# Two attention layers on one core: the places at which the next pair's q, k and v are quantized in the first image's attention

## The chip, the cores and the metric

The kernel runs on one core of one Trainium2 chip. The metric is the device time of one execution in microseconds (us); the time before is the median of 3 runs. One further execution was recorded by the hardware profiler, and all profile lines come from it. Its engines are TensorE (PE, with its weight loads PEld), VectorE (DVE), ScalarE (ACT), GpSimd (POOL) and SyncE (SP), which here issues most of the DMAs.

## The reference

Two layers over 8 images of 512 channels and 1024 positions. Layer 0 is an attention with 8 heads of 64 channels whose q, k and v are each fake-quantized with one scale for the whole tensor; layer 1 is an attention with one head of 512 channels. Cut to what matters here:

```python
def fake_quant(x):                       # scale and zero point of the whole tensor
    scale = max((xmax - xmin) / 255, 1e-8)
    zp = round(-xmin / scale)
    return (clip(round(x / scale) + zp, 0, 255) - zp) * scale

# layer 0
h = group_norm(x, gn_w, gn_b)
q, k, v = split(einsum('oc,bct->bot', qkv_w, h) + qkv_b)   # per head
q, k, v = fake_quant(q), fake_quant(k), fake_quant(v)
w = softmax(einsum('bct,bcs->bts', q * s, k * s))
a = einsum('bts,bcs->bct', w, v)
x = x + einsum('oc,bct->bot', proj_w, a) + proj_b
# layer 1
t = group_norm(x, ...)
x = x + proj(softmax(q1(t) @ k1(t).T / sqrt(512)) @ v1(t))
```

## The kernel before

Since the quantizing scale needs the whole tensor, the kernel first computes q, k and v of all images, writes them to DRAM in float32 and keeps running extremes (the first 577 us of the trace). Then come layer 0's attention and layer 1. They are interleaved: the attention of image b+1 is given out in small portions between the matmuls of layer 1 of image b. For the first image there is no layer 1 to interleave with yet, and its attention runs by itself. It is accompanied only by `fold`, which multiplies layer 1's weight matrices together.

The attention works in *units*. A unit is (image b, head pair j, half hf of the queries, key tile s): 128 keys against 512 queries, for two heads at once. A pair thus has 16 units, and an image 4 pairs. For each unit:

- `scores` (TensorE): two matmuls of the pair's quantized k and q into `st`, which has two buffers; then ScalarE's exponential from `st` into `pt`, 128x1024 float32.
- `split`: `pt` is cut into two float16 parts in the tile `two`. The high part is a cast, on ScalarE, or on GpSimd where s % 4 is 2, or on VectorE where s is 5; the low part, the remainder `pt - high`, is always VectorE's. In the first image units with s % 4 of 3 are `plain`: their `pt` is used in float32 (tile `aside`) and no split is made.
- `over_keys` (TensorE): the products `av` of `two` with the quantized v (float32 `vf` for plain units). `totals` (TensorE): the row sums `sm`.

In `attention`, one turn of the loop takes four units u to u+3 through `over_keys` and `totals`, and at the same time computes the scores of units u+6 to u+9 and splits them. So scores run six to eight units ahead of the products. The first scores of the next pair therefore come in the last turns of this one.

`load_pair(b, j, u)` prepares the next pair while this one runs; u is the number of this pair's first unit. It fetches q and k (512 KB each) by SP into tiles `raw`, of which there are two, and lays out the quantizing. q, k and v each take two VectorE steps over 128x1024: `quant` (scale and round, in place in `raw`) and `quant2` (clip, into bfloat16 q and k or float16 v). v of the first image has a third, `whole`, which writes the rows of the plain units in float32 into `vf`. That makes seven steps. `fetch_v` loads v into the tile that q has left; the next pair's q then goes into k's tile and its k into v's.

What sets the order of this work depends on the phase. In the first image's attention, `InOrder.strict` is set and `InOrder.planned` is not: the instructions on each engine stay in the order in which the program writes them. Small pieces of work wait in the list `dealt`, each with the number of the unit from which it may go. Each `split(u)` calls `deal(u)`, which takes one piece, the first in the list whose number has been reached (and `fetch_v` with it if it stands next). In this way the quantizing steps, the divide by the row sums (`ao`), the sums' reciprocals (`rcs`) and steps of `fold` are scattered among the remainders on VectorE. `settle("qk")` in `scores` gives out whatever of q and k is left when a new pair begins; `settle("qv")` does it for v.

For later images, `InOrder.planned` is set: a planner with costs and due times orders the same work through `dve.later`. SP's DMAs, too, run in order of its queue; a load waits there until its tile is free, and what stands behind it waits as well.

## Time and profile before

| | us |
|---|---|
| median of 3 runs (lowest, highest) | 2619.14 (2615.93, 2619.39) |
| profiled execution, its own time | 2616.86 |
| span of its trace | 2615.1 |
| TensorE busy | 2532.9, 97% |
| VectorE busy | 1905.7, 73% |
| ScalarE busy | 1360.2, 52% |
| GpSimd busy | 189.2, 7% |
| mean granted TensorE clock | 0.989 of full |
| first scores of the first image | 585.62 |
| first scores of its pairs 1, 2, 3, and of the next image | 617.63, 650.79, 684.44, 717.21 |
| first projection matmul of image 0 | 741.76 |

A line of the timeline gives the start in us, the duration in us, the engine, the line of the program, the operation, the tile written and the tile read, their shapes, how many instructions are merged, and in brackets the idle time before it and what ended it. Nearly all engine instructions carry the line of a helper (L91 or L209), so they are told apart by the tiles. A line of the busy times by stretch gives the stretch, its length, the busy time of TensorE, its weight loads, VectorE, ScalarE and GpSimd with the number of instructions, the granted TensorE clock, the DMA engines' mean busy share and GB/s. Durations of one instruction overlap a little with the next one's start, so that the distance between starts is shorter than a duration.

### The profile page before, as it was taken

The page shows a single profiled execution, that of the slowest core. Times are in us where ns is not written, and L with a number is a line of the kernel's source. Part 1 is how long each engine was busy: PE and PEld are TensorE (multiplying, and loading weights), DVE is VectorE, ACT ScalarE, POOL GpSimd, SP SyncE. Part 2 cuts the span into 40 slices and gives each one's busy share as a digit, 9 for nine tenths or more (in the row PEclk, how much of TensorE's full clock was granted, in tenths as well). Part 3 has the DMA queues.
Part 4 walks back from the last instruction along what each step waited for, and adds up shares of the span by engine and source line. Part 5 has one row for each costly group of instructions (what it writes and reads, how often), then busy time and mean ns, then how long its engine had stood idle before and what let it go on. Part 6 is the DMA issues. An engine that isn't in the chain of part 4 may idle for free.

```text
span 2615.1 us, 38713 instructions
## 1 busy us (share of the span) xinstructions
PE 2532.9 (97%) x15670; PEld 1749.2 (67%) x15670; DVE 1905.7 (73%) x2748; ACT 1360.2 (52%) x1696; POOL 189.2 (7%) x153
## 2 busy tenths in 40 slices
PE   7999999997888999999999999999999999999998
PEld 4788888872235775776677577757766775777687
DVE  7888776667776777877777777778777776776544
ACT  3222222217765674666566566746665765664121
POOL 0000000001100001000100010010001000100000
PEclk9999999998899999999999999999999999999999
DMA  4343333332221232223212322322232123212211
GB/s 173 128 166 128 122 128 121 118 140 81 70 94 42 69 103 82 86 79 108 96 51 78 118 85 63 109 82 86 73 110 97 54 78 117 86 42 87 91 37 38
DMA packets 156013, 243.09 MB, mean 93 GB/s; under 512 B 26544, under 2 KB 93104, under 8 KB 154288
## 3 DMA queue, kind: packets, MB, share of 16 engines
q1 hardware_dynamic: 125264, 182.81, 21.3%
q10 hardware_dynamic: 30560, 57.71, 6.5%
q8 instruction: 125, 2.05, 0.3%
q14 instruction: 64, 0.52, 0.1%
HBM read 153.64 MB, written 86.28 MB: 92 GB/s over the span
## 4 chain that ended last, share of the span: by engine, by line
PE 86%; DVE 5%; ACT 3%; issue 2%; DMA 1%; POOL 0%; SPq 0%; ACTq 0%; DVEq 0%
PE s L209 15%; PE o L209 14%; PE qkps L209 12%; PE pj L209 8%; PE av L209 8%; PE v2ps L209 7%; PE g L209 7%; PE vps L209 6%; PE st L209 4%; PE sm L209 4%; DVE two L91 2%; ACT pt L91 1%; PE fold L209 1%; ACT two L91 0%; DVE acc L91 0%
## 5 line engine op out<-in xcount | busy, mean ns | idle before, releaser
L91 ACT ACTIVATE pt<-st,esc 128x1024 f32<-128x1024 f32 x496 | 527.8, 1114 | 367.6 <-PE st L209 351.7
L91 DVE TENSOR_TENSOR two<-pt,two 128x1024 f16<-128x1024 f32 x496 | 597.1, 1217 | 166.6 <-POOL two L1050 108.4
L91 ACT CAST two<-pt 128x1024 f16<-128x1024 f32 x358 | 362.2, 1054 | 13.6 <-PE sm L209 8.2
L1050 POOL CAST two<-pt 128x1024 f16<-128x1024 f32 x128 | 166.7, 1302 | 1568.2 <-ACT pt L91 779.8
L209 PE MATMUL av<-two,v 128*32 128x512 f16 x3968 | 248.0, 385 | 9.5 <-DVE v L91 9.5
L209 PE MATMUL s<-g,h 128*128 128x256 f32 x1024 | 233.4, 380 | 0.0
L209 PE MATMUL pj<-ao,wp 128*128 128x512 f32 x512 | 224.2, 595 | 2.4 <-DVE ao L91 2.0
L209 PEld LDWEIGHTS s<-g,h 128*128 128x128 f32 x1024 | 192.9, 190 | 31.0 <-issue 4.3
L209 PE MATMUL st<-q,k 64*128 64x512 bf16 x1024 | 165.7, 388 | 37.4 <-DVE k L91 23.3
L91 ACT ACTIVATE u_ring<-qkps,qkbt 128x512 f32<-128x512 f32 x89 | 61.1, 687 | 250.4 <-PE qkps L209 235.6
L209 PEld LDWEIGHTS <-v 128*32 128x32 f16 x3968 | 91.5, 96 | 148.8 <-issue 66.1
L209 PEld LDWEIGHTS pj<-ao,wp 128*128 128x128 f32 x512 | 96.0, 190 | 124.4 <-issue 112.5
L209 PE MATMUL s<-g,sums 128*128 128x256 f32 x768 | 178.5, 381 | 0.2 <-DVE p L91 0.2
L209 PE MATMUL o<-p,v 128*128 128x256 f32 x768 | 175.2, 382 | 1.0 <-DVE p L91 1.0
L209 PEld LDWEIGHTS o<-p,v 128*128 128x128 f32 x768 | 144.3, 190 | 27.1 <-issue 5.7
L209 PEld LDWEIGHTS s<-g,sums 128*128 128x128 f32 x768 | 144.6, 190 | 24.3 <-issue 4.1
L209 PEld LDWEIGHTS <-k 64*128 64x128 bf16 x1024 | 34.4, 94 | 169.6 <-issue 142.0
L209 PE MATMUL sm<-two,ones 128*32 128x512 f16 x1984 | 137.0, 381 | 0.0
L209 PE MATMUL qkps<-half,w_low 128*128 128x512 f32 x480 | 132.2, 398 | 2.3 <-DVE half L91 2.3
L209 PE MATMUL qkps<-half,w_high 128*128 128x512 f32 x480 | 133.7, 401 | 0.0
L209 PE MATMUL qkps<-half,w_mix 128*128 128x512 f32 x480 | 131.2, 396 | 1.1 <-DVE half L91 1.1
L209 PE MATMUL g<-h,wa 128*128 128x256 f32 x512 | 120.8, 384 | 0.0
(221 smaller groups left out, 3834.8 us busy)
## 6 DMA issues: line engine op xcount, KB each, us to landing
rs<-rs_d SPq DMA_DIRECT2D x76, 256.0 KB
x<-in_x_dram SPq DMA_DIRECT2D x32, 512.0 KB
q_d<-wa SPq DMA_DIRECT2D x32, 512.0 KB
k_d<-wa SPq DMA_DIRECT2D x32, 512.0 KB
v_d<-v_ring SPq DMA_DIRECT2D x32, 512.0 KB
raw<-q_d SPq DMA_DIRECT2D x32, 512.0 KB
raw<-k_d SPq DMA_DIRECT2D x32, 512.0 KB
x_d<-h SPq DMA_DIRECT2D x64, 256.0 KB
```

The source lines that it names most:

```text
L91: ins = self.latest = op(*args, **kw).ins
L209: ins = nc.tensor.matmul(ps, lhsT=lhsT, rhs=rhs, **kw).ins
L1050: copy(two[:, 0], pt)
```

## The change

Three numbers in `quants`, in the branch that is taken when the work is dealt out in program order. q's two steps move from splits 12 and 13 after the pair's start to 7 and 8, k's from 14 and 15 to 9 and 10, and v's three from 19, 20 and 21 to 15, 16 and 17. `fetch_v`, which goes with q's second step, moves from 13 to 8. The branch serves the first image's attention, that is, the steps for its pairs 1 to 3 and for the first pair of the next image.

```diff
@@ -969,9 +969,9 @@
                     if u is None or InOrder.planned:
                         dve.later(name, 0.7, work, pe.t + 12.0, 45.0)
                     else:
-                        dealt.append((u + (12, 14, 19)[i] + n, name, work))
+                        dealt.append((u + (7, 9, 15)[i] + n, name, work))
                         if (i, n) == (0, 1):
-                            dealt.append((u + 13, "qk", fetch_v))
+                            dealt.append((u + 8, "qk", fetch_v))
 
             def fetch_v():
                 if len(raws) == 2:
```

The order of instructions that follows from it: on VectorE, k's last step stands right behind the remainder of unit 10 of the pair that runs, where it stood behind the remainder of unit 14 (pairs 0 to 3; the steps for the second pair of the next image keep their places, since other pieces stand ahead of them in the list). v's steps stand around the next pair's first two remainders, where they stood around its units 2 to 4. On SP's queue, the next pair's k load comes ahead of the two loads of `h` and of the row sums' small transfers in pair 1, and ahead of the row sums' transfers in pair 2. The orders on TensorE, ScalarE and GpSimd are the same as before.

## The prediction

> **What bounds the kernel now.** I read the page first (TensorE busy 97% of the span, and 86% of the chain that ended last), then the waits of the stretch from 577 to 760 us, the only one in which the edited branch deals its work out, then the timelines of TensorE and VectorE there, and last the busy times by stretch. In the waits, the columns are total us, times, longest:

> ```profile
> ACT pt L91 <- PE st L209: 40.6, 10, 13.5
> DVE two L91 <- ACT two L91: 34.0, 13, 5.3
> ...
> PE st L209 <- DVE k L91: 23.0, 4, 5.9
> ```

> TensorE waits four times, 5.7 to 5.9 us each, for the quantized k of the next pair. ScalarE's and VectorE's long waits are the echo: while no scores come they run dry. TensorE's timeline around the second of the four, and a later piece of the same fold product:

> ```profile
> 644.24 0.61 PE L209 MATMUL sm<-two,ones 128*32 128x512 f16 x8
> 650.79 0.61 PE L209 MATMUL st<-q,k 64*128 64x512 bf16 x2 [5.95 <-DVE k L91]
> 651.33 2.08 PE L209 MATMUL fold<-wn_v 128*128 128x512 f32 x2
> ...
> 663.01 1.13 PE L209 MATMUL fold<-wn_v 128*128 128x512 f32 x2
> ```

> The fold product takes 2.08 us right after the wait and 1.13 us later. The reason is the granted clock, the last column before DMA and GB/s here; both stretches hold the same work (two scores, one fold step, one split unit and one plain unit of av, and their sums):

> ```profile
> 650.79:656.99 6.20, 6.20 (x26) 1.39 (x27) 2.06 (x2) 4.65 (x5) 0.00 (x0) 0.50 0.26 85
> 666.01:669.33 3.32, 3.32 (x30) 0.96 (x27) 3.29 (x4) 3.21 (x4) 0.83 (x1) 1.00 0.35 101
> ```

> So a wait costs twice: its own length, and then 6.20 - 3.32 = 2.88 us of half clock. VectorE's timeline shows why k is late:

> ```profile
> 644.90 1.52 DVE L91 TENSOR_SCALAR q<-raw,bhi 128x1024 bf16<-128x1024 f32 x1
> 646.34 0.68 DVE L91 CAST two<-pt 128x1024 f16<-128x1024 f32 x1
> 647.05 1.23 DVE L91 TENSOR_TENSOR two<-pt,two 128x1024 f16<-128x1024 f32 x1
> 648.19 0.75 DVE L91 TENSOR_SCALAR raw<-raw,rcp 128x1024 f32<-128x1024 f32 x1
> 648.86 1.22 DVE L91 TENSOR_TENSOR two<-pt,two 128x1024 f16<-128x1024 f32 x1
> 649.99 0.75 DVE L91 TENSOR_SCALAR k<-raw,bhi 128x1024 bf16<-128x1024 f32 x1
> 650.65 1.28 DVE L91 SCALAR_TENSOR_TENSOR ao<-ao,scl,rs 128x1024 f32<-128x1024 f32 x1
> 656.07 1.22 DVE L91 TENSOR_TENSOR two<-pt,two 128x1024 f16<-128x1024 f32 x1 [4.14 <-ACT two L91]
> ```

> When TensorE comes for k (644.85), VectorE still has six operations to do, k the last, with remainders of units 13 and 14 between them that nobody needs for another six units. It has no pause before, then 4.14 us with nothing to do. The k data are not late: their load was issued at 633.18 and the DMA went quiet by 637.

> [...] clock 0.50 after waits of 5.7 us, and none after waits of 1.1 us (at 739.03). [...] The q step above (1.52 us, not 0.75) started while GpSimd's cast of 644.53 ran[...].

> **The change, part by part.** [...] Nothing is added or removed; VectorE, ScalarE, GpSimd and TensorE run as many instructions as before. [...]

> Removed waits: 5.68 + 5.95 + 5.68 + 5.69 = 23.0 us.

> Half clock after them: from the first scores of a pair to those of units 2 and 3 the timeline takes 5.72, 6.20, 4.75 and 5.42 us; at full clock 3.32. The sum over 3.32 each is 2.40 + 2.88 + 1.43 + 2.10 = 8.8 us. TensorE alone would thus gain 31.8 us.

> It can't keep all of that, since the other engines have to follow. Busy times by pair, in the order TensorE, weights, VectorE, ScalarE, GpSimd:

> ```profile
> 585.62:617.63 32.01, 22.89 (x165) 6.58 (x164) 23.61 (x31) 25.14 (x26) 4.74 (x4) 0.87 0.12 40
> 617.63:650.79 33.16, 27.05 (x248) 8.52 (x249) 24.81 (x29) 25.40 (x28) 5.42 (x4) 0.91 0.40 128
> 650.79:684.44 33.65, 27.80 (x236) 7.92 (x237) 27.64 (x38) 25.47 (x28) 4.56 (x4) 0.86 0.26 79
> 684.44:717.21 32.77, 26.59 (x236) 7.89 (x238) 22.80 (x25) 24.71 (x27) 5.07 (x4) 0.92 0.23 66
> 717.21:741.76 24.55, 20.75 (x214) 7.18 (x214) 17.93 (x20) 22.92 (x25) 4.07 (x3) 0.91 0.27 90
> ```

> New length of each piece, as the largest of TensorE's own time and the other engines' busy time. Pair 0: 32.01 - 5.68 = 26.3. Pair 1: TensorE 33.16 - 5.95 - 2.40 = 24.8, ScalarE 25.4, VectorE 25.9 (its work counted from one pair's first remainder to the next, 622.91 to 656.07): 25.9. Pair 2: TensorE 33.65 - 5.68 - 2.88 = 25.1, VectorE 27.6: 27.6. Pair 3: TensorE 32.77 - 5.69 - 1.43 = 25.65: 25.7. The last piece: TensorE 24.55 - 2.10 = 22.45, ScalarE 22.9: 22.9. Together 128.4 against 156.1: 27.7 us. No two engines mesh without a gap, so I take off 0.5 us at each of the four pair ends (TensorE's waits inside an undisturbed pair are 0.2 to 0.6): 26 us.

> Does k come in time? The remainder of unit 10 ends, in the trace of before, 4.4, 1.75, 2.1 and 4.4 us ahead of the four waits' starts. Four quantizing steps of 0.66 (start to start) now come ahead of its successor: 2.65 us[...]. Pairs 0 and 3 keep a margin of about 1 to 1.8. In pair 1 two steps on wa (0.6 and 1.45) fall behind k, so it keeps about 1. In pair 2 nothing falls behind, and 0.6 to 1.4 us of wait stay. That is part of the 2.5 us that pair 2 has above TensorE's own time, not extra.

> What is delayed: remainders of units 8 to 10, by up to 2.65 us. Those of units 8 and 9 of pair 0 ended at 605.46 and were first read at 610.48, so 5 us are there; if that cover is gone, TensorE stands for the excess. Those of units 12 to 14 come earlier by as much.

> Loads, on SP's queue in order: v's (issued 613.29, moved by 617: 3.7 us) now follows q's second step some 10 us earlier; the next q's (617.61, done by 621) follows k. The next k's is moved past the two 1 MB loads of h and the small loads of the row sums; it waits for v's last step and makes those loads wait too. They are released by the fold's row product at 625.19 and needed for the projection at 751, so 0 us. From v's last step to k's first there are eight units, about 8 x 1.6 = 13 us, for a load of under 4: 0 us; bounds 0 and 2 us each, if h's 2 MB share the engines. [...] The divide by the row sums keeps its place behind the same DMA chain. From the projection on, the order on every engine is the old one and is only shifted.

> The sum: 2616.86 (span 2615.1 and 1.8 around it) less 26 = 2590.9. The profiled time lies below the median, 2619.14, inside the runs' 2615.93 to 2619.39; half of that offset put back gives **2592**.

> **Rivals.** (1) *VectorE takes over the wait.* At 27.6 of 27.6 us it has no slack in pair 2 and little in pair 1, so remainders come late and TensorE stands for them[...]. For it: VectorE ran without a pause from 638 to 652. Against it: its 38 us of pauses in this stretch. If two of four pair ends keep a wait of 3.5 us and 2.3 of slow clock: 26 - 11.6 = 14 us gained, 2604. (2) *Nothing moves*: something else ends the wait at the same time, such as ScalarE's exponentials, whose scores buffers are two. Against it: ScalarE itself idles 5.7 us in each of the four. 2618. (3) *Slower: the k load.* VectorE works in order, so if k's data were not there at split 9, all remainders would queue behind the step, and the pairs would be longer than now. Place: the next k's load, released by v's last step. Price: from 13 us after release on, each us costs one per pair; it eats the gain of 6.5 per pair at 19.5 and loses beyond. At 22 us, 4 x 2.5 = 10 lost: 2627. The loads seen take under 4 us, so it is remote.

> **How the numbers follow.** Forecast 0.68, own range 2587 to 2597[...]; rival 1 0.24, spread over 2597 to 2611; rival 2 0.04; rival 3 0.04. I take 2585 to 2604, which leaves out the far part of rival 1 and the last two. This kernel's measurements can tell about 0.2%, 5 us, from no change: faster 0.92, same 0.04, slower 0.04.

> **What would show it.** Right: waits of scores for k gone or under 2 us, largest at the end of pair 2; the clock near 1.00 from 600 to 740; pairs of 26 to 28 us; ScalarE and VectorE busy above nine tenths. Wrong: av products waiting for remainders by over 1 us (rival 1), a quantizing step waiting for a DMA (rival 3), or a projection that does not start about 26 us earlier than at 741.76.

## The result, and the profile after

Four runs of the changed kernel have a median of 2594.31 us (2592.55 to 2595.38), beside 2618.69 us (2615.93 to 2619.39) before: a ratio of 0.9908, 95% interval 0.9891 to 0.9925. The profiled execution took 2592.55 us against 2616.86, so 24.3 us less.

The stage in question runs from the first scores of the first image to its first projection matmul. It took 156.1 us before and takes 131.0 now. The busy times by pair of the changed kernel, in the order TensorE, weights, VectorE, ScalarE, GpSimd, then the clock (the last line is the stretch just after the end of pair 2):

```profile
585.52:611.73 26.21, 22.77 (x165) 6.58 (x165) 20.73 (x29) 24.45 (x26) 4.58 (x4) 0.87 0.21 73
611.73:637.29 25.56, 24.79 (x253) 8.19 (x250) 23.44 (x26) 25.02 (x29) 4.90 (x5) 1.00 0.43 140
637.29:666.16 28.87, 25.40 (x240) 7.75 (x237) 28.66 (x40) 25.70 (x29) 7.18 (x5) 1.00 0.27 79
666.16:693.04 26.88, 26.52 (x237) 7.78 (x238) 24.38 (x26) 24.05 (x27) 3.95 (x4) 0.94 0.40 112
693.04:716.48 23.44, 18.84 (x219) 6.88 (x215) 22.33 (x23) 23.34 (x26) 5.15 (x4) 1.00 0.23 81
...
666.16:671.07 4.91, 4.91 (x26) 1.16 (x27) 4.88 (x6) 3.48 (x4) 0.00 (x0) 0.65 0.72 216
```

The pairs took between 32.0 and 33.7 us and now take between 25.6 and 28.9. In each of the pieces at least one of TensorE, VectorE and ScalarE is now busy for over nine tenths of the time. Pair 2 is the longest, and VectorE is busy for 28.66 of its 28.87 us.

The waits of the changed kernel from 577 to 735 us, which is a little past the end of the stage:

```profile
ACT pt L91 <- PE st L209: 18.6, 6, 14.5
...
DVE two L91 <- ACT two L91: 10.7, 8, 2.9
...
ACT pt L91 <- DVE two L91: 2.9, 4, 1.4
...
PE st L209 <- DVE k L91: 1.9, 1, 1.9
```

Of the 23.0 us in which TensorE waited for k, one wait of 1.9 us is left, and the echoes on ScalarE and VectorE shrink with it. (ScalarE's longest wait, 14.5 us, lies behind the stage, where no scores are due; so did the 13.5 us before.) The third line is new in the stage: ScalarE has to wait for VectorE's remainders before it can reuse a `pt` buffer. Three of those four waits lie in pair 2; the fourth, of 0.46 us, stands behind the stage in both kernels.

TensorE's timeline at the end of pair 2, and VectorE's at the same place:

```profile
663.63 0.60 PE L209 MATMUL sm<-two,ones 128*32 128x512 f16 x8
666.16 0.39 PE L209 MATMUL st<-q,k 64*128 64x512 bf16 x2 [1.93 <-DVE k L91]
666.48 1.64 PE L209 MATMUL fold<-wn_v 128*128 128x512 f32 x2
```

```profile
662.69 1.22 DVE L91 TENSOR_TENSOR two<-pt,two 128x1024 f16<-128x1024 f32 x1
663.83 0.75 DVE L91 TENSOR_SCALAR raw<-raw,rcp 128x1024 f32<-128x1024 f32 x1
664.61 1.50 DVE L91 TENSOR_SCALAR k<-raw,bhi 128x1024 bf16<-128x1024 f32 x1
666.03 1.21 DVE L91 TENSOR_TENSOR two<-pt,two 128x1024 f16<-128x1024 f32 x1
```

VectorE's operations follow each other without a gap, and k's last step takes 1.50 us instead of 0.75: GpSimd's cast, which ran from 664.52 to 665.56, covers its start. After the wait the fold product takes 1.64 us instead of 1.12, and the clock over the next 4.91 us is 0.65.

The gain of the stage is 156.14 - 130.96 = 25.2 us. One more microsecond of it goes at the projection, where TensorE waits 1.95 us for the last `ao` in both kernels (the first line is of before, the next two are of the changed kernel):

```profile
746.56:751.50 4.94, 4.56 (x10) 1.82 (x10) 4.90 (x6) 0.00 (x0) 0.00 (x0) 1.00 0.18 53
```

```profile
716.48:734.33 17.85, 15.90 (x37) 6.51 (x34) 13.28 (x16) 3.33 (x5) 0.00 (x0) 0.90 0.38 130
721.27:726.20 4.93, 4.93 (x8) 2.15 (x9) 4.89 (x6) 0.00 (x0) 0.00 (x0) 0.65 0.19 55
```

After the same wait the clock was 1.00 before and is 0.65 now. The projection with what surrounds it, up to the next scores, takes 17.85 us where it took 16.85. So 25.2 - 1.0 = 24.2 us, and the profiled executions differ by 24.3.

### The profile page after: what moved, and what is told of

Same layout as the page of the kernel before. It is cut to its first block, busy times and chain, and to the rows that moved or that the text cites. A ratio compares the mean times of both kernels' runs of the same rounds, so it can differ in the third digit from the quotient of the medians.

```text
span 2590.7 us, 38714 instructions
## 1 busy us (share of the span) xinstructions
PE 2527.7 (98%) x15670; PEld 1749.0 (68%) x15670; DVE 1909.7 (74%) x2748; ACT 1359.1 (52%) x1696; POOL 191.0 (7%) x153
## 3 DMA queue, kind: packets, MB, share of 16 engines
q8 instruction: 125, 2.05, 0.3%
## 4 chain that ended last, share of the span: by engine, by line
PE 85%; DVE 5%; ACT 3%; issue 2%; DMA 1%; POOL 0%; ACTq 0%; SPq 0%; DVEq 0%
PE s L209 15%; PE o L209 14%; PE qkps L209 12%; PE pj L209 9%; PE av L209 8%; PE v2ps L209 7%; PE g L209 6%; PE vps L209 6%; PE st L209 4%; PE sm L209 4%; DVE two L91 2%; ACT pt L91 1%; DVE h L91 1%; PE fold L209 0%; ACT two L91 0%
## 5 line engine op out<-in xcount | busy, mean ns | idle before, releaser
L91 ACT ACTIVATE pt<-st,esc 128x1024 f32<-128x1024 f32 x496 | 528.6, 1115 | 348.0 <-PE st L209 331.0
L91 DVE TENSOR_TENSOR two<-pt,two 128x1024 f16<-128x1024 f32 x496 | 599.3, 1222 | 138.7 <-POOL two L1050 103.8
L91 ACT CAST two<-pt 128x1024 f16<-128x1024 f32 x358 | 362.4, 1055 | 13.3 <-PE sm L209 8.0
L209 PE MATMUL av<-two,v 128*32 128x512 f16 x3968 | 247.5, 384 | 9.3 <-DVE v L91 9.2
L209 PE MATMUL s<-g,h 128*128 128x256 f32 x1024 | 233.4, 380 | 0.0
L209 PE MATMUL pj<-ao,wp 128*128 128x512 f32 x512 | 225.6, 599 | 2.0 <-DVE ao L91 2.0
L209 PEld LDWEIGHTS s<-g,h 128*128 128x128 f32 x1024 | 192.9, 190 | 31.0 <-issue 4.3
L91 ACT ACTIVATE u_ring<-qkps,qkbt 128x512 f32<-128x512 f32 x89 | 61.2, 687 | 250.5 <-PE qkps L209 233.6
L209 PEld LDWEIGHTS <-v 128*32 128x32 f16 x3968 | 91.6, 96 | 147.8 <-issue 65.0
L209 PE MATMUL st<-q,k 64*128 64x512 bf16 x1024 | 164.6, 385 | 18.8 <-ACT pt L91 11.0
L209 PEld LDWEIGHTS pj<-ao,wp 128*128 128x128 f32 x512 | 96.6, 191 | 124.7 <-issue 113.1
L209 PE MATMUL s<-g,sums 128*128 128x256 f32 x768 | 178.4, 381 | 0.2 <-DVE p L91 0.2
L209 PE MATMUL o<-p,v 128*128 128x256 f32 x768 | 175.2, 382 | 1.0 <-DVE p L91 1.0
L209 PEld LDWEIGHTS o<-p,v 128*128 128x128 f32 x768 | 144.3, 190 | 27.1 <-issue 5.7
L209 PEld LDWEIGHTS s<-g,sums 128*128 128x128 f32 x768 | 144.7, 190 | 24.2 <-issue 4.1
L209 PE MATMUL sm<-two,ones 128*32 128x512 f16 x1984 | 136.7, 381 | 0.0
L209 PEld LDWEIGHTS <-k 64*128 64x128 bf16 x1024 | 34.7, 94 | 148.3 <-issue 142.0
L209 PE MATMUL qkps<-half,w_low 128*128 128x512 f32 x480 | 132.1, 398 | 2.3 <-DVE half L91 2.3
L209 PE MATMUL qkps<-half,w_high 128*128 128x512 f32 x480 | 133.9, 401 | 0.0
L209 PE MATMUL qkps<-half,w_mix 128*128 128x512 f32 x480 | 131.2, 395 | 1.1 <-DVE half L91 1.1
L209 PE MATMUL g<-h,wa 128*128 128x256 f32 x512 | 120.8, 384 | 0.0
```

The costliest lines, as they stand in the source:

```text
L91: ins = self.latest = op(*args, **kw).ins
L209: ins = nc.tensor.matmul(ps, lhsT=lhsT, rhs=rhs, **kw).ins
```

## The experiments

The median of before, run beside the first four, was 2618.69 us (19 runs); beside the next two 2617.92 (7 runs); beside the last two 2619.38 (7 runs). The time at which the first scores start differs from execution to execution, 585.2 to 589.5 us, with work that no edit here touches. The length of the stage is therefore a better measure of an edit than the total. It is read from the single profiled execution of each kernel, and the clock in it counts: the changed kernel and after_again are the same program, and their stages differ by 2.5 us.

| kernel | stage, us | its pairs 0 to 3 and last piece, us | median, us | ratio to before, 95% |
|---|---|---|---|---|
| before | 156.1 | 32.0, 33.2, 33.7, 32.8, 24.6 | 2618.69 | |
| the changed kernel | 131.0 | 26.2, 25.6, 28.9, 26.9, 23.4 | 2594.31 | 0.9908 (0.9891 to 0.9925) |
| qk_only | 131.3 | 25.0, 25.6, 31.7, 25.6, 23.5 | 2594.22 | 0.9908 (0.9891 to 0.9925) |
| v_only | 157.5 | 31.5, 32.7, 33.9, 33.9, 25.5 | 2619.89 | 1.0002 (0.9993 to 1.0011) |
| two_splits | 134.9 | 26.7, 27.7, 29.7, 27.1, 23.9 | 2597.96 | 0.9919 (0.9903 to 0.9936) |
| kept_busy | 148.7 | 31.3, 31.5, 31.3, 31.4, 23.3 | 2612.21 | 0.9974 (0.9963 to 0.9985) |
| fold_later | 129.1 | 26.4, 25.6, 26.3, 27.2, 23.6 | 2590.52 | 0.9898 (0.9882 to 0.9915) |
| fold_later_chain | 128.9 | 26.2, 25.6, 26.3, 27.2, 23.6 | 2592.15 | 0.9904 (0.9887 to 0.9920) |
| after_again | 128.5 | 25.0, 25.6, 28.9, 25.6, 23.4 | 2593.99 | 0.9902 (0.9886 to 0.9919) |
| after_filled | 130.1 | 26.1, 25.6, 28.9, 25.6, 24.0 | 2592.49 | 0.9895 (0.9879 to 0.9912) |

**Which of the moved steps carries the gain.** qk_only moves q and k and leaves v; v_only does the reverse:

```diff
-                        dealt.append((u + (12, 14, 19)[i] + n, name, work))
+                        dealt.append((u + (7, 9, 19)[i] + n, name, work))
                         if (i, n) == (0, 1):
-                            dealt.append((u + 13, "qk", fetch_v))
+                            dealt.append((u + 8, "qk", fetch_v))
```

> The changed kernel with v's three steps back at splits 19 to 21; q, k and the v load stay at their new places. My theory: all of the gain comes from k being ready, so the four waits of scores for k stay under 2.5 us, and the stretch from the first scores of image 0 (585.5) to its first projection matmul takes 129 to 133 us (before 156.1, changed 131.0); time within 3 us of the changed kernel's. Rival (the earlier v belongs to it, since the next pair's k loads into the tile that v leaves): quantizing k waits for its load at splits 9 and 10, and the stretch takes 138 us or more.

```diff
-                        dealt.append((u + (12, 14, 19)[i] + n, name, work))
+                        dealt.append((u + (12, 14, 15)[i] + n, name, work))
```

> The kernel before with only v's three steps moved from splits 19 to 21 to 15 to 17; q, k and the v load stay. My theory: k's last step is where it was, so the four waits stay at 5 to 7 us with half clock after them, and the stretch takes 154 to 159 us; time that of the kernel before within 3 us. Rival (v's share of the gain is a third or more): 148 us or less.

v_only keeps all four waits for k (5.69, 5.75, 5.98 and 5.69 us) and its time. qk_only has the whole gain of the total. The rival, quantizing steps that wait for a load, does not show in its waits. Its pair 2, however, is 2.8 us longer than in the changed kernel, because there v comes too late. For k one wait of 1.4 us is left in its stage, for v there are two, and TensorE's timeline shows the longer one:

```profile
650.58 1.90 PE L209 MATMUL av<-two,v 128*32 128x512 f16 x16 [3.23 <-DVE v L91]
```

The products `av` of pair 2 stand for v, 3.23 us. Moving v with q and k takes this wait away. That the stage of qk_only is as short as the changed kernel's all the same is due to the clock in that execution: it was 1.00 in pairs 0 and 3, which the changed kernel passed at 0.87 and 0.94, and that gave back 1.2 us in each. Beside after_again, with 1.00 in both, qk_only's stage is 2.8 us longer. The medians, of four runs each, are too coarse to show 2.8 us.

**How far the move has to go.** two_splits moves the steps by two splits:

```diff
-                        dealt.append((u + (12, 14, 19)[i] + n, name, work))
+                        dealt.append((u + (10, 12, 17)[i] + n, name, work))
                         if (i, n) == (0, 1):
-                            dealt.append((u + 13, "qk", fetch_v))
+                            dealt.append((u + 11, "qk", fetch_v))
```

> All of the change, but by two splits instead of five and four: q at 10, k at 12, v at 17, v load at 11. My theory: of the six VectorE operations that k waited for, the cast and the remainders of units 13 and 14 (0.68 + 1.14 + 1.14 = 3.0 us) now come after it, so waits of 2.7 us stay, with part of the half clock: 156.1 - 4 x 3.0 - 4 x 0.7 = 141 us for the stretch, 138 to 144. Rival (the gain grows evenly with the number of splits): two fifths of 25 us, so 146 us; rival (any move suffices): 131 us.

The gain is larger than I expected: the stage is 134.9, not 138 to 144. The waits for k at the four pair ends are 1.36, 2.15, 2.98 and 1.36 us, where I had worked out 2.7 each from the remainders that stay ahead of k. The sum left out VectorE's own pauses. At the end of pair 0, ahead of which neither kernel has a wait for k, VectorE stood idle for 2.31 us in before (at 610.59, for a cast of ScalarE) and stands idle for 1.23 us in two_splits (at 613.27): 1.1 us of the steps that moved ahead went into that pause and delayed nothing. At the end of pair 2, where VectorE has no such pause shortly before, the wait is 2.98 us, close to the sum. A pair that starts without a long wait may also let VectorE reach the next k sooner, but these runs don't show that apart. What the whole move adds to two splits is 134.9 - 131.0 = 4 us, clock included.

**What the half clock costs by itself.** kept_busy is the kernel before with small matmuls of ones by ones ahead of each pair's first scores. They go to a bank that is otherwise free and nothing reads them; k comes as late as before.

```diff
                     settle("qk")
+                    if 0 < u <= 64:
+                        warm = bank(f"warm_{u}")
+                        for _ in range(18):
+                            mm(warm[:, 0:P], lhsT=ones, rhs=ones, start=True, stop=True)
```

> The kernel before with 18 more matmuls of 128 by 128 ones ahead of the first scores of each pair, into a bank that nobody reads, some 4.3 us in a place where TensorE waits 5.7 us anyway. My theory of the two prices: the scores still wait for k, but the clock stays at 1.00 after the waits, so that each pair saves 1.4 to 2.9 us and the stretch takes 147 to 150 us. Rival (half clock costs nothing there, because the other engines are behind anyway and set the pace): 155 us or more.

TensorE's timeline of kept_busy at the second pair end, where before had a wait of 5.95 us and then a fold product of 2.08 us:

```profile
644.88 4.29 PE L209 MATMUL warm<-ones 128*128 128x128 f32 x36
650.90 0.39 PE L209 MATMUL st<-q,k 64*128 64x512 bf16 x2 [1.73 <-DVE k L91]
651.22 1.13 PE L209 MATMUL fold<-wn_v 128*128 128x512 f32 x2
```

The scores start as late as they did, but the fold product takes 1.13 us. The stage falls by 156.1 - 148.7 = 7.4 us. Of this 0.7 us lies in pair 0, ahead of the first filled wait, and is not the filling's. The four pieces behind the waits fall by 1.7, 2.4, 1.4 and 1.2 us, together 6.7. This is the half clock behind the four waits, with the waits still there; the prediction's sum for it was 8.8. The median fell by 6.5 us.

**Is pair 2 bound by VectorE?** fold_later deals the row product of the second fold (`i` is 1), four reductions and what follows them, out from unit 51 on, so that some 3.6 us of VectorE's work move from pair 2 into pair 3:

```diff
             def through(i):
...
-                    dealt.append((0, "fold", lambda e=e: dve.tensor_tensor_reduce(
+                    dealt.append(((0, 51)[i], "fold", lambda e=e: dve.tensor_tensor_reduce(
...
-                dealt.append((0, "fold", last))
+                dealt.append(((0, 51)[i], "fold", last))
```

> The changed kernel, with the four row-product reductions of the fold and the pieces that finish its row z and wide (about 3.6 us of VectorE) dealt out from unit 51 on instead of unit 0, which takes them from pair 2 into pair 3. Theory (VectorE's work is what sets pair 2, and the k wait that is left at its end comes from it): pair 2 falls from 28.87 us to about 26, the 1.93 us wait for k at its end and the half clock after it go, pair 3 stays at 26 to 27 since VectorE had 2.5 us of slack there; the stage from the first scores to the first projection matmul falls from 130.96 to 127 to 128.5, total 2589 to 2592. Rival (something else sets pair 2, or the work only moves the wait on to pair 3): the sum of pairs 2 and 3 stays at 55 to 56, stage 130 to 131, total as the changed kernel.

The busy times of fold_later in pairs 2 and 3:

```profile
637.11:663.42 26.31, 25.09 (x240) 7.66 (x236) 25.95 (x28) 24.88 (x29) 6.30 (x5) 1.00 0.35 94
663.42:690.62 27.20, 25.17 (x240) 7.65 (x236) 26.99 (x37) 25.25 (x28) 5.91 (x5) 1.00 0.31 95
```

VectorE's busy time in pair 2 falls from 28.66 to 25.95 us and the pair from 28.87 to 26.31, and its wait for k at the end is gone. So VectorE's work sets the length of pair 2; that part of the theory is shown. The sum is not what I expected: pair 3 now holds the work, VectorE is busy for 26.99 of its 27.20 us, and a wait for k of 1.50 us has appeared at its end. Pairs 2 and 3 together take 53.5 us against 55.8, and the stage, 129.1, is above the 127 to 128.5 that I expected. As after_again shows below, 1.2 of these 2.2 us are clock (53.51 against 55.75), so the moved work is worth about 1 us. The medians, 2590.52 and 2594.31, have overlapping ratios, so that fold_later is not shown to be the faster of the two. The projection took 16.85 us here, with the clock at 1.00 after a wait of 1.96 us.

**The chain before the projection.** fold_later_chain is fold_later with the last pair's sums and divide given out earlier. It also joins `keep`, the stores of the fold's result `wm`, to the last of the four steps on `wm`, so that the stores take no turn of their own in `dealt`; the diff here leaves that part out:

```diff
                     if InOrder.planned:
                         dve.later("ao", elements(1100), divide, dve.t + 7.0, 20.0)
+                    elif (b, j) == (0, PAIRS - 1):
+                        dealt.insert(0, (u + 14, "ao", divide))
                     else:
                         dealt.append((u + 20, "ao", divide))
...
-                    dealt.append((u + 12, "ao", spread))
+                    dealt.append((u + (10 if (b, j) == (0, PAIRS - 1) else 12), "ao", spread))
```

> As fold_later, and the last pair's chain of row sums, transfer and divide is given out earlier (the transfer of the sums from unit +10 instead of +12 after it, the divide ahead of other pieces from +14 instead of +20). Theory (the half clock at the projection's start in the changed kernel, 17.85 us against 16.85 for the same piece before, comes from the 1.95 us wait for the last ao): the wait goes, the piece to the first scores of the next image's second pair falls to 15 to 16 us, total 4 to 7 us under the changed kernel, 2587 to 2590. Rival (the half clock comes from elsewhere, or the projection then waits for other data such as h): the piece stays at 17 to 18 us and the total is that of fold_later.

The wait for `ao` goes, and TensorE runs sixteen projection matmuls in a row. Then it waits longer than before for something else:

```profile
714.47 7.13 PE L209 MATMUL pj<-ao,wp 128*128 128x512 f32 x16
724.26 8.83 PE L209 MATMUL pj<-ao,wp 128*128 128x512 f32 x16 [2.65 <-DVE h L91]
```

VectorE takes the projection's results into `h`, and the first of these stands behind the remainders and quantizing steps for the next image, until 723.46. The piece takes 18.55 us, 0.7 more than in the changed kernel, and the median is no better than that of fold_later. My rival had this case; the theory had not looked at who is next in VectorE's order. Since `keep` moved too, the comparison with fold_later is not of the chain alone.

**Does a short wait bring half clock?** after_again is the changed kernel once more, and after_filled has six small matmuls ahead of pair 3's first scores:

> The changed kernel itself once more, beside the runs of before on the same chip. Theory (the half clock after its waits of 1.9 us is decided by the order of work in it, which is the same in each execution): 0.65 over the 4.9 us after the wait at the end of pair 2 and again after the wait for ao at the projection, stage 130.5 to 131.5, total 2592 to 2595. Rival (whether a short wait brings half clock differs from execution to execution): at least one of the two stretches has a clock of 1.00, and the total is 1 to 2.6 us lower.

```diff
                     settle("qk")
+                    if u == 48:
+                        warm = bank(f"warm_{u}")
+                        for _ in range(6):
+                            mm(warm[:, 0:P], lhsT=ones, rhs=ones, start=True, stop=True)
```

> The changed kernel with six small matmuls of ones by ones into a free bank ahead of pair 3's first scores, which fill most of TensorE's 1.93 us wait there. They compute nothing that is used. Theory (pair 3's 26.88 us hold about 1.6 us of half clock that the short wait brought): the wait that is left is about 0.5 us, the clock after it 1.00, pair 3 falls to 25.2 to 25.8, pair 2 stays at 28.5 to 29, stage 129 to 130, total 1 to 2 us lower. Rival (pair 3 is set by ScalarE and VectorE, so that a slow TensorE costs nothing there): pair 3 stays at 26.5 to 27.

The busy times of after_again, over the same stretches of work as in the changed kernel's profile (pairs 0, 2 and 3, the projection's piece, and after the wait for `ao`):

```profile
589.51:614.52 25.01, 20.02 (x165) 6.11 (x164) 20.70 (x29) 24.34 (x26) 4.21 (x4) 1.00 0.23 73
...
640.09:668.95 28.86, 25.39 (x240) 7.76 (x236) 28.65 (x40) 25.70 (x29) 7.17 (x5) 1.00 0.29 81
668.95:694.59 25.64, 25.11 (x237) 7.66 (x238) 24.39 (x26) 23.98 (x27) 4.69 (x4) 1.00 0.41 117
...
718.03:734.88 16.85, 14.47 (x38) 5.83 (x34) 13.17 (x16) 3.33 (x5) 0.00 (x0) 1.00 0.41 138
722.82:727.75 4.93, 4.56 (x10) 1.82 (x10) 4.89 (x6) 0.00 (x0) 0.00 (x0) 1.00 0.17 47
```

The waits are the same, 1.93 and 1.95 us, and the clock stays at 1.00 after both (over the 4.91 us from 668.95 on as well). The rival holds: whether a wait of that length brings half clock differs between executions of one kernel. (The last section shows what goes with it.) Pair 0 is 1.2 us shorter, pair 3 1.2 and the projection's piece 1.0; pair 2, whose clock was 1.00 in both, takes 28.86 against 28.87. The total was not lower, 2594.42 us, since the stage began 4.0 us later in this execution.

after_filled has 0.39 us left of the wait at the end of pair 2 and a pair 3 of 25.63 us, but after_again has 25.64 with the whole wait. So this run doesn't show that the filling did it. It shows a stretch of 0.65 elsewhere: over 4.85 us from 716.15 on, with no wait of TensorE above 1.10 us shortly before. TensorE was busy for 1.69 of the 3.40 us ahead of it. At the same place in after_again it was busy for the same 1.69 of 3.40 (from 713.21 on), and the clock stayed at 1.00. v_only and two_splits have the slow stretch there too, before, the changed kernel and qk_only don't.

## Why the prediction was right

- **The waits.** 23.0 us of waits for k were to go, but for 0.6 to 1.4 us at the end of pair 2. One wait is left, there, of 1.93 us. The term was 0.5 us too small at its upper end, which took one step as 0.78 us longer, my estimate: q's second step was that much longer in before while a GpSimd cast ran (1.52 us at 644.90, against 0.74 to 0.75 for k's). In the changed kernel k's last step took 1.50. The term was worked out from before's margin at the remainder of unit 10; in the changed kernel VectorE runs behind through much of the pair, as ScalarE's three new waits for `two` show.
- **The half clock after them.** 8.8 us by the sum of before's stretches, 6.7 by kept_busy. The term was 2.1 us too large, the largest part of it in the last piece (2.10 against 1.2). That did little harm: only pair 3's share, 1.43 us against a measured 1.4, enters the forecast, since in pairs 1 and 2 and in the last piece another engine was the larger.
- **The pieces as the largest of the engines' times.** With the 0.5 us put on at each pair end the forecast stands at 26.8, 26.4, 28.1, 26.2 and 22.9. The profile has 26.2, 25.6, 28.9, 26.9 and 23.4. No piece is off by more than 0.9 us, and the sum, 130.4, is off by 0.6. Where after_again has no half clock, pair 0 is 25.0 and pair 3 25.6: the engines mesh better than I allowed, and the allowance stood in for the clock that came back. That the sum came out so close is in part luck: against after_again's profile pair 0 is off by 1.8 us.
- **Pair 2.** VectorE as its bound was right and is shown by fold_later. The term was mis-sized by its busy time, 28.66 us instead of 27.6. Two of `wa`'s steps, 0.67 and 0.68 us, now run in pair 2 (at 637.93 and 641.11); the prediction saw that such steps fall behind k in pair 1, and did not add them to the next pair. They make 1.35 us, which is more than the 1.06 us that were missing; what else changed nearly cancels. Operations that take longer while a cast of GpSimd runs are in both kernels: before's pair 2 has three (1.52, 1.13 and 1.53 us at 658.96, 665.86 and 678.54, each started 0.1 to 0.4 us after the start of a cast), the changed kernel's has four (1.94, 2.05, 2.05 and 1.50 us at 639.24, 643.50, 651.15 and 664.61, each started while a cast ran). Among these are two remainders of 1.94 and 2.05 us where others take 1.2, and one cast of GpSimd takes 3.06 us where the other four of the pair take 1.04 to 1.23. Against the same operations elsewhere in the two profiles (0.68, 0.34 and 0.75; 1.21, 1.28, 1.21 and 0.75 us) the three are 2.4 us longer and the four 3.1. The difference, 0.7 us, is among what nearly cancels.
- **Loads.** The next k loads were issued at 619.16, 648.78, 676.10 and 701.27 us, over 10 us ahead of their use, and no quantizing step waited for one. The first of them stood on SP's queue for 11.3 us, until v's last step (`vf`, 618.00 to 619.13) had freed its tile, and h's two loads behind it were issued at 619.57; from 623 to 628 us the DMA engines' mean busy share was 0.96 or more. The third rival had no part in it.
- **"From the projection on, the order on every engine is the old one and is only shifted".** The order is, and the wait for `ao` is even the same 1.95 us, but its cost isn't: 1.0 us of half clock came in. The prediction had read from one place in the trace of before that a wait of 1.1 us leaves the clock alone (1.09 us at 739.03, and 1.00 over the next 2.97 us), and let the same hold for this one, which that place did not show. The trace of before held a slow stretch after waits of at most 1.70 us, at the start of pair 0 (below), which the prediction passed over.
- **The rivals.** VectorE did take over a wait, in one of the four pair ends and for 1.9 us with about 1.2 us of slow clock after it; the first rival had asked for two of them with 3.5 and 2.3, which was my estimate.
- **The signs.** The waits, and the projection's start 25.3 us earlier, came as named. Others came only in part: the clock was 0.94 in pair 3 and 0.90 in the projection's piece, pairs 1 and 2 lie just outside 26 to 28 us (25.6 and 28.9), and VectorE was busy for 0.79 of pair 0, not over nine tenths.

The predicted gain of 26 us stands against 24.3: 25.2 in the stage, less the 1.0 at the projection. By after_again's profile the stage gains 156.1 - 128.5 = 27.6 us, so the forecast lies between the two executions. Half of the offset between profile and median had been put back, which gave 2592; the median is 2594.31. The range of 2587 to 2597 around it was my estimate.

## What to carry to other kernels

When a wait is taken away, work out each piece anew as the largest of the engines' busy times, not as the old length less the wait: with 0.5 us put on at each pair end, that gave the new length of every piece here within 0.9 us in one profile and within 1.8 us in the other. Then look at which engine sets each piece, and who stands next in its order: moving VectorE's work out of pair 2 brought up a wait in pair 3, and hurrying `ao` brought up one for `h`. Differences of 1 to 3 us in one profile are read beside a second profile of the same kernel, since the clock alone moved the stage from 131.0 to 128.5 us.

## What was not expected of the hardware

The prediction had taken short waits as harmless to the clock. In these runs the clock after them differed, between kernels and between two executions of one kernel:

```profile
663.54:666.95 3.41, 1.48 (x19) 0.50 (x8) 3.38 (x4) 2.28 (x3) 1.04 (x1) 1.00 0.68 192
666.95:670.37 3.42, 3.42 (x20) 0.71 (x22) 3.38 (x5) 2.42 (x3) 0.00 (x0) 0.50 0.87 246
```

```profile
664.75:668.16 3.41, 2.28 (x29) 0.67 (x28) 3.38 (x5) 3.41 (x5) 0.85 (x1) 1.00 0.81 220
668.16:671.57 3.41, 2.62 (x22) 0.89 (x26) 3.38 (x4) 2.01 (x3) 0.19 (x1) 1.00 0.77 177
671.57:674.99 3.42, 3.42 (x42) 1.02 (x34) 3.42 (x5) 3.42 (x5) 0.15 (x1) 1.00 0.62 223
```

- In the first, nearly the whole wait falls into one step, TensorE is busy for 1.48 us of it, and the next step is slow from end to end. In the second, the same wait is cut in two at 668.16, TensorE is busy for 2.28 and 2.62 us, and no slow step follows. Over all ten profiles, from 585 to 745 us, a step at full clock with TensorE busy for 1.46 us or less was followed by a slow one in 18 of 18 cases, and one with 1.74 us or more in none of 408. Between 1.48 and 1.71 us it was 7 of 14. In the profiles of before and of the changed kernel alone these are 7 of 7, none of 68, and 1 of 3.
- So in these profiles a slow step goes with how little TensorE worked in the step before it; neither the length of the last wait nor the order of work alone tells it. This is read from the traces; no run here moved the steps on purpose. The wait for `ao` (1.46 us busy in the changed kernel, 1.50 in after_again) and the lull of after_filled (1.70) lie at or in the range where both occurred; what decides there stays open.
- One such stretch cost 1.0 to 1.2 us, by the pieces of the changed kernel and of after_again.
